# First batch's side steps moved to the side bank and VectorE, and the squares of the bound moved from GpSimd to ScalarE

## The chip, the cores and the metric

The kernel runs on one core of one Trainium2 chip, in a single launch. The metric is the device time of that launch in microseconds (us); less is better. A core has five engines with a queue each: TensorE (PE in the profile, with its weight loads as PEld), VectorE (DVE), ScalarE (ACT), GpSimd (POOL) and SyncE (SP), which only issues DMAs here. Each works through its own queue in program order and they meet through semaphores.

## What is computed

One transformer block over 4 sequences of 1024 tokens with 256 features, in float32: attention with 16 heads of 16, then a gated feed-forward with two hidden layers of 1024 and ternary weights. Cut to what matters:

```python
x = x + _layernorm(attn(_layernorm(x), Wqkv, Wout))
x = x + _layernorm(ffn(_layernorm(x), w1, s1, w2, s2, h1, ..., w3, s3))

def attn(x, Wqkv, Wout):
    q, k, v = split_heads(x @ Wqkv.T)                 # 16 heads of 16
    scores = einsum('bhqd,bhkd->bhqk', q, k) / 4
    e = exp(clip(scores - max(scores), -50, 50))
    return merge_heads((e / (sum(e) + 1e-6)) @ v) @ Wout.T

def ffn(x, ...):
    h = silu(x @ w1.T * s1) * (x @ w2.T * s2)
    h = gelu(h @ h1.T * hs1)
    h = gelu(h @ h2.T * hs2)
    return h @ w3.T * s3
```

The fast path takes the exponential without subtracting the maximum. It therefore also works out, for each batch, a bound on the scores from the squared norms of the rows of q and k, and counts a miss where that bound is too large. If anything was missed, a slow general path is run after the fast one.

## The kernel before, in words

**Stages.** Attention runs for batches 0 to 3, one after the other, and then the feed-forward for the eight half batches. In attention a batch has 4 groups of 4 heads, and 2 halves of 512 queries; a group and a half make a *unit* of 16 *tiles*. A tile (`exponentials`, lines 444 to 452) is two score matmuls of TensorE into one PSUM buffer `s` of 128x1024 (tag "big", three buffers), and one exponential of ScalarE from it into a ring. `weigh` (line 459) multiplies the exponentials with the values into the unit's accumulator `acc`; `rise` (line 468) keeps running maxima on VectorE.

**Turns.** The main loop (lines 858 to 878) goes by turns. In each, it issues the scores and exponentials of three new tiles, the maxima and the weighing of those of the turn before, and then calls `side.take()` once. `Side` (lines 551 to 578) holds chains of small steps. A call of `take` goes through all chains in order, and runs a chain's next step if as many turns have passed since its last step as the step's `gap` says. Steps marked as TensorE steps (the default) are limited to one per turn over all chains; others are free. So `gap` 0 means in the same turn as the step before, and `gap` 1 a turn later.

**The steps of a batch.** `prologue(b, space, copy)` (line 271) makes a batch's steps: normalising the rows (`gather`, `root`, `apply`), transposing them (`transposes`, line 305), projecting them to values (`values`, line 315) and to q and k (`project`, line 324), and the bound (`flags`, lines 334 to 393). Each of those that uses TensorE takes a PSUM place from `space(name)` and brings its result to SBUF by `copy`: `to_scalar` (line 266, on ScalarE) or `to_vector` (line 269, on VectorE). `project` makes two results of one product: `hi`, rounded, by `copy`, and `lo`, the rest, always on VectorE (line 328).

Two places are in use for these steps. `misc` is a single bank of its own (tag "misc", one buffer). The other is one of the three "big" buffers that the scores use. Batches 1 to 3 pass `misc` and `to_vector` (line 586): their steps run as side steps while the batch before is attended. Batch 0 passes a "big" buffer and `to_scalar` (line 819). Its normalising, transposing, its first q and k and `v[0]` run before the first tile, straight from lines 827 to 840; the rest (`v[1]` to `v[3]`, the second half of the features of q and k in four projections, and the flags) are side steps of the first units (lines 844 and 845). Between them stand the steps `slots`, in which GpSimd spreads the values into the layout `vaug` that `weigh` reads.

**The bound.** For each half of 512 tokens there are four squares (`kinds`: q and k, two blocks of features), each a product of a 128x512 `hi` with itself into a bfloat16 tile `sq` of four buffers, on GpSimd (line 338). `bound` (lines 354 to 361) sums them over the head's features by four matmuls, and VectorE takes maxima (`norm`). In the end `gauge` and `flag` compare. In the list of line 401 the squares have gap 0 and are no TensorE steps, so the four of a half are issued in one turn; `bound` follows three turns later at the earliest, when the turn's TensorE step is free.

**Other work in the same turns.** At the end of a unit VectorE copies the accumulator (`o`), and in the next turn `divide` (lines 470 to 493) takes one "big" buffer, transposes maxima and sums with TensorE and divides on VectorE. At the end of a batch `ending` projects the result and adds it to x. All through the first three batches `check_weights` (lines 237 to 263) checks that the feed-forward weights survive rounding: GpSimd loads and casts, VectorE counts (line 257). SyncE copies q and k into the stacked layout of the scores by DMA.

Of the kernel before, what the change touches and what calls it, by code (L numbers as in the profile page):

```python
# [9 lines left out]
F32 = mybir.dt.float32  # L10
# [3 lines left out]
AF = mybir.ActivationFunctionType  # L14
ALU = mybir.AluOpType
# [3 lines left out]
P = 128  # L19
# [16 lines left out]
NQ = 512  # L36
# [4 lines left out]
@with_exitstack  # L41
def tile_attention_ffn_block(ctx: ExitStack, tc: tile.TileContext, x, wqk, wv, wo, w1, w1s, w2, w2s, h1, h1s, h2, h2s, w3, w3s, out):

    nc = tc.nc
    B, S, D = x.shape
    bad = ctx.enter_context(tc.tile_pool(name="flag", bufs=1)).tile([1, 1], I32, name="bad")
    tile_fast(tc, x, wqk, wv, wo, w1, w1s, w2, w2s, h1, h1s, h2, h2s, w3, w3s, out, bad)
    failed = nc.values_load(bad[0:1, 0:1], min_val=0, max_val=1 << 24)
    with tc.If(failed > 0):
        tile_general(tc, x, wqk, wv, wo, w1, w1s, w2, w2s, h1, h1s, h2, h2s, w3, w3s, out)
# [46 lines left out]
def tile_fast(ctx: ExitStack, tc: tile.TileContext, x, wqk, wv, wo, w1, w1s, w2, w2s, h1, h1s, h2, h2s, w3, w3s, out, bad):  # L115
    nc = tc.nc
# [19 lines left out]
    def pieces(h, view):  # L136

        t, n = NH + (TPQ - 1) * h, TPQ * h
        return (slice(n, n + 1), view[:, h : h + 1, :]), (slice(n + 1, n + TPQ), view[:, t : t + TPQ - 1, :])

    def load_x(b, halves=range(NH)):
        view = x[b].rearrange("(t p) d -> p t d", p=P)
        for h in halves:
            for at, tokens in pieces(h, view):
                nc.sync.dma_start(out=xs[b][:, at, :], in_=tokens)
# [26 lines left out]
    ps = ctx.enter_context(tc.tile_pool(name="ps", bufs=3, space=PSUM))  # L172
# [4 lines left out]
    with ExitStack() as actx, ExitStack() as rctx:  # L177
# [56 lines left out]
        def misc(name):  # L234
            return ps_misc.tile([P, NQ], F32, tag="misc", name=name)
# [35 lines left out]
        def prologue(b, space, copy):  # L271
# [6 lines left out]
            def gather(h, i):  # L278
                def run():
                    if h == i == 0:  # L280
                        st["xT"] = work.tile([P, DC, S], F32, tag="xT", name=f"xT_{b}", bufs=1)
                    st["mv", h] = norms.gather(rows(h)[i : i + 2], i, st.get(("mv", h)))

                return run

            def root(h):
                def run():
                    st["ln", h] = norms.root(st["mv", h])

                return run  # L290

            def apply(h, i0):
                def run():
                    if i0 == 0:
                        st["xn"] = work.tile([P, TPQ, D], F32, tag="xn", name="xn", bufs=1)
                    for i in range(i0, i0 + 2):
                        norms.apply(st["xn"][:, i, :], rows(h)[i], st["ln", h], i)

                return run

            def transposes(h, c):
                def run():
                    pt = space(f"pt_{b}_{h}_{c}")
                    for i in range(TPQ):
                        nc.tensor.transpose(pt[:, i * P : (i + 1) * P], st["xn"][:, i, c * P : (c + 1) * P], ident)
                    copy(st["xT"][:, c, h * NQ : (h + 1) * NQ], pt)

                return run

            def values(t0):  # L310
                def run():
                    pv = space(f"pv_{b}_{t0}").rearrange("p (t d) -> p t d", d=D)
                    for i in range(2):
                        for c in range(DC):
                            nc.tensor.matmul(pv[:, i, :], st["xT"][:, c, (t0 + i) * P : (t0 + i + 1) * P], wv_sb[:, c, :], start=c == 0, stop=c == DC - 1)  # L315
                    copy(cv[:, t0 : t0 + 2, :], pv)

                return run

            def project(w, m, h):  # L320
                def run():
                    pp = space(f"p{w}_{b}_{m}_{h}")
                    for c in range(DC):
                        nc.tensor.matmul(pp, wqk_sb[:, c, w, HPT * m : HPT * (m + 1), :], st["xT"][:, c, h * NQ : (h + 1) * NQ], start=c == 0, stop=c == DC - 1)  # L324
                    hi, lo = (cq[w, m, k][:, h * NQ : (h + 1) * NQ] for k in ("hi", "lo"))
                    scale = 1.0 if w else 1.0 / math.sqrt(DH)
                    copy(hi, pp, scale)
                    nc.vector.scalar_tensor_tensor(lo, pp, scale, hi.bitcast(F32), ALU.mult, ALU.subtract)

                return run  # L330

            kinds = [(w, m) for w in range(2) for m in range(DC)]

            def squares(w, m, h):
                def run():
                    sq = st["sq", w, m] = work.tile([P, NQ], BF16, tag="sq", name="sq", bufs=4)
                    hi = cq[w, m, "hi"][:, h * NQ : (h + 1) * NQ].bitcast(F32)
                    nc.gpsimd.tensor_tensor(sq, hi, hi, ALU.mult)

                return run  # L340

            def total(m):
                def run():
                    if m == 0:
                        st["norm"] = work.tile([P, NT], F32, tag="norm", name=f"norm_{b}", bufs=1)
                        st["sum"] = work.tile([P, DC], F32, tag="sum", name="sum", bufs=1)
                        st["sum2"] = work.tile([P, DC], BF16, tag="sum2", name="sum2", bufs=1)
                    t = st["sum"][:, m : m + 1]
                    nc.vector.tensor_reduce(t, cq[1, m, "hi"].bitcast(F32), AX.X, ALU.add)
                    nc.gpsimd.tensor_tensor(st["sum2"][:, m : m + 1], t, t, ALU.mult)  # L350

                return run

            def bound(h):


                def run():
                    pn = space(f"pn_{b}_{h}")
                    for k, (w, m) in enumerate(kinds):
                        nc.tensor.matmul(pn[SLOT * k : SLOT * (k + 1), :], heads_bf, st["sq", w, m], start=True, stop=True)  # L360
                    nc.vector.tensor_reduce(st["norm"][:, TPQ * h : TPQ * (h + 1)], pn.rearrange("p (t n) -> p t n", n=P), AX.X, ALU.max)

                return run
# [31 lines left out]
            norm = [[Step(gather(h, i), 1, False) for i in range(0, TPQ, 2)] + [Step(root(h), 0, False)] for h in range(NH)]  # L395
            xt = [[Step(apply(h, i), 1, False) for i in range(0, TPQ, 2)] + [Step(transposes(h, c), 1) for c in range(DC)] for h in range(NH)]
            qk = [[[Step(project(w, m, h), 1) for w in (1, 0)] for h in range(NH)] for m in range(DC)]
            v = [Step(values(t), 1) for t in range(0, NT, 2)]
            flags = [Step(total(m), 1, False) for m in range(DC)]
            for h in range(NH):  # L400
                flags += [Step(squares(w, m, h), 0, False) for w, m in kinds] + [Step(bound(h), 3)]
            return norm, xt, qk, v, flags + [Step(gauge, 0, False), Step(flag, 1)]

        def copies(g, w, c0=0, c1=S):
# [14 lines left out]
        def stack(b, g):  # L419
            for w in (1, 0):  # L420
                for copy in copies(g, w):
                    copy(nc.sync)
            stacked[g % 2] = b, g
# [159 lines left out]
        def begin(b):  # L583

            if b + 1 < B:
                norm, xt, qk, v, flags = prologue(b + 1, misc, to_vector)

                qk1 = sum(qk[1], [])
                qk1[0].gap = 3
                later["rest"] = v, qk1 + [Step(lambda: side.add(flags), 0, False)]  # L590

                later["chain"] = side.add([Step(lambda: None, 0 if b else 4, False)] + sum((norm[h] + xt[h] for h in range(NH)), []) + sum(qk[0], []))
# [210 lines left out]
        def feed_forward():  # L803
# [12 lines left out]
                chain = side.add(finish(n, ffn["a"]), True)  # L816
            side.flush()

        norm, xt, qk, v, flags = prologue(0, lambda n: ps.tile([P, 2, NQ], F32, tag="big", name=n)[:, 0, :], to_scalar)

        queues = [nc.scalar] + [nc.gpsimd, nc.sync] * 3 + [nc.gpsimd]

# [15 lines left out]
                        step.run()  # L838
        stacked[0] = 0, 0
        v[0].run()  # L840
        load_x(1)
        stack(0, 1)
        load_rest()
# [14 lines left out]
        while weighed < len(tiles):  # L858
            n = made
            make(n + TURN - side.borrowed)  # L860
            if made == len(tiles):
                n = made
# [3 lines left out]
            while weighed + 2 <= n:  # L866
                b, g, h, c, _ = tiles[weighed]
# [252 lines left out]
```

## Time and profile before

| | us |
|---|---|
| median of three runs | 1350.21 (1348.44 to 1350.24) |
| the profiled execution | 1349.57 |
| its span, first to last instruction | 1347.8 |
| the stage before the first tile | 0 to 25 |
| attention | 25 to 671 |
| feed-forward | 671 to 1347.8 |

Busy times of the engines in these stages (us), from the table of stretches:

| stage | PE | DVE | ACT | POOL |
|---|---|---|---|---|
| 0 to 25 | 19.4 | 11.0 | 7.3 | 13.2 |
| 25 to 671 | 598.5 | 406.6 | 488.8 | 126.5 |
| 671 to 1347.8 | 661.5 | 318.4 | 189.0 | 19.5 |

The lines of the profile give a start, a length, an engine, the line of the program, the operation, what it writes and reads by the program's names, and how many like it were merged ("x6"). In brackets stands how long the engine had been idle before it, and what ended that. A busy TensorE isn't TensorE at its peak: the length of a matmul includes time in which it shares the array with the next. The squares in groups:

```profile
L338 POOL TENSOR_TENSOR sq<-cq1hi 128x512 bf16<-128x512 f32 x8 | 11.4, 1430 | 0.0
L338 POOL TENSOR_TENSOR sq<-ck0hi 128x512 bf16<-128x512 f32 x8 | 11.0, 1371 | 0.0
L338 POOL TENSOR_TENSOR sq<-ck1hi 128x512 bf16<-128x512 f32 x8 | 10.6, 1329 | 0.0
L338 POOL TENSOR_TENSOR sq<-cq0hi 128x512 bf16<-128x512 f32 x8 | 8.3, 1036 | 2.3 <-PE pn L360 2.3
```

Behind the bars stand the group's busy time in us, the mean of one in ns, and the idle time before them.

### The profile page before, as it was taken

To read this page: it belongs to the slowest core of one execution; us is meant where nothing else is said; L and a number is where in the kernel's file an instruction comes from. 1 tells how busy PE (TensorE), PEld (TensorE's weight loads), DVE (VectorE), ACT (ScalarE), POOL (GpSimd) and SP (SyncE) were. 2 spreads that over 40 slices of the span, in tenths; PEclk is the share of its full clock that TensorE was granted. 3 is DMA by queue.
4 is the path that set the end of the run, shared out by engine and by line. 5 is a ranking of instruction groups with operands and counts; after the bars stand their busy time and mean duration, and the time that the engine had idled before them with its cause. 6 is when DMAs were issued, how large, how long until landed. Compare 5 with 4: busy or idle time off the path is not lost.

```text
span 1347.8 us, 18771 instructions
## 1 busy us (share of the span) xinstructions
PE 1279.4 (95%) x7042; PEld 799.8 (59%) x7042; DVE 736.0 (55%) x1554; ACT 685.1 (51%) x822; POOL 159.2 (12%) x198
## 2 busy tenths in 40 slices
PE   7889999899899999989999999999999999999995
PEld 3333434333343434323378888888888888888885
DVE  3485568665697565735573453635537354362623
ACT  4576687676778678888842231413214142231410
POOL 6151133210521003000000000000000000000000
PEclk9999999899999999999999999999999999999998
DMA  4674344533445432236130000000000000000000
GB/s 132 150 176 113 78 111 93 141 90 69 130 104 141 95 50 49 48 65 198 36 153 1 1 16 0 17 1 0 16 1 16 1 1 17 0 16 1 17 0 19
DMA packets 38662, 79.62 MB, mean 59 GB/s; under 512 B 11296, under 2 KB 21152, under 8 KB 38560
## 3 DMA queue, kind: packets, MB, share of 16 engines
q1 hardware_dynamic: 30672, 53.66, 18.3%
q0 software_dynamic: 7360, 24.12, 5.4%
q8 instruction: 58, 0.95, 0.3%
q10 hardware_dynamic: 528, 0.52, 0.2%
q14 instruction: 44, 0.36, 0.1%
HBM read 28.98 MB, written 15.73 MB: 33 GB/s over the span
## 4 chain that ended last, share of the span: by engine, by line
PE 75%; DVE 12%; ACT 7%; issue 2%; POOL 2%; DMA 1%; SPq 1%; ACTq 0%; POOLq 0%; DVEq 0%
PE ph L697 35%; PE acc L459 13%; PE s L451 8%; ACT e L452 5%; PE pz L750 4%; PE p L324 4%; PE pg L697 3%; PE py L516 2%; PE pv L315 2%; DVE sg L713 2%; DVE top L468 2%; PE po L480 1%; DVE ha_lo L702 1%; DVE st L93 1%; DVE o L269 1%
## 5 line engine op out<-in xcount | busy, mean ns | idle before, releaser
L452 ACT ACTIVATE e<-s 128x1024 f32<-128x1024 f32 x512 | 484.9, 1033 | 144.4 <-PE s L451 128.5
L459 PE MATMUL acc<-e,vaug 128*32 128x512 f32 x2048 | 258.3, 607 | 1.8 <-POOL vaug L429 1.8
L733 ACT ACTIVATE a<-ph,h_scale 128x512 f32<-128x512 f32 x128 | 81.0, 685 | 306.9 <-PE ph L697 306.9
L451 PE MATMUL s<-sq,sk 64*128 64x512 f32 x1024 | 196.4, 453 | 26.1 <-ACT e L452 20.4
L697 PE MATMUL ph<-hb_lo,h 128*128 128x512 f32 x512 | 199.4, 389 | 0.0
L697 PE MATMUL ph<-hb_hi,h 128*128 128x512 f32 x512 | 199.4, 389 | 0.0
L451 PEld LDWEIGHTS s<-sq,sk 64*128 64x128 f32 x1024 | 87.5, 186 | 162.8 <-ACT e L452 120.1
L468 DVE TENSOR_TENSOR top<-top,e 128x512 f32<-128x512 f32 x192 | 146.2, 761 | 30.1 <-ACT e L452 24.1
L103 POOL TENSOR_TENSOR rstd<-ve,minus_half 128x4 f32<-128x4 f32 (+1 forms) x33 | 37.5, 1135 | 796.5 <-DVE ve L101 796.5
L459 PEld LDWEIGHTS acc<-e,vaug 128*32 128x32 f32 x2048 | 49.6, 109 | 108.8 <-issue 98.5
L734 DVE CAST ha_hi<-a 128x512 fp32r<-128x512 f32 x64 | 27.1, 424 | 157.9 <-ACT a L733 157.9
L697 PEld LDWEIGHTS ph<-hb_lo,h 128*128 128x128 f32 x512 | 96.1, 188 | 20.1
L697 PEld LDWEIGHTS ph<-hb_hi,h 128*128 128x128 f32 x512 | 96.1, 188 | 20.1
L697 PE MATMUL ph<-ha_hi,sq 128*128 128x512 f32 x256 | 101.9, 398 | 0.4
L697 PE MATMUL ph<-ha_lo,sq 128*128 128x512 f32 x256 | 99.8, 390 | 0.0
L697 PE MATMUL ph<-ha_lo,sk 128*128 128x512 f32 x256 | 99.7, 390 | 0.0
L697 PE MATMUL ph<-ha_hi,sk 128*128 128x512 f32 x256 | 99.7, 390 | 0.0
L713 DVE SCALAR_TENSOR_TENSOR sg<-pg,w_scale,sg 128x512 f32<-128x512 f32 x64 | 47.1, 745 | 47.9 <-ACT sg L711 47.8
L711 ACT ACTIVATE sg<-pg,w_scale 128x512 f32<-128x512 f32 x64 | 43.3, 688 | 56.6 <-DVE ha_lo L702 48.4
L734 DVE CAST hb_hi<-a 128x512 fp32r<-128x512 f32 x64 | 27.0, 422 | 82.2 <-ACT a L733 82.2
L324 PE MATMUL p<-xT,wqk_sb 128*128 128x512 f32 x128 | 64.6, 631 | 1.2 <-ACT xT L266 1.2
L697 PEld LDWEIGHTS ph<-ha_hi,sq 128*128 128x128 f32 x256 | 48.2, 188 | 12.7 <-DVE sg L713 3.4
(147 smaller groups left out, 1689.7 us busy)
## 6 DMA issues: line engine op xcount, KB each, us to landing
w<-in_h_dram POOLq DMA_DIRECT2D x16, 512.0 KB, 4.7
h_r<-wr POOLq DMA_DIRECT2D x16, 512.0 KB, 3.6
sk<-ck1hi SPq DMA_DIRECT2D x64, 64.0 KB, 2.3
sk<-ck1lo SPq DMA_DIRECT2D x64, 64.0 KB, 2.3
sq<-cq1hi SPq DMA_DIRECT2D x64, 64.0 KB, 2.3
sq<-cq1lo SPq DMA_DIRECT2D x64, 64.0 KB, 2.3
h<-h_r SPq DMA_DIRECT2D x8, 512.0 KB, 6.5
sk<-ck0hi SPq DMA_DIRECT2D x56, 64.0 KB, 2.3
```

Of the source, the lines that this page charges most:

```text
L103: nc.gpsimd.tensor_tensor(rstd[:, :n], ve[:, :n], self.minus_half[:, :n], ALU.pow)
L324: nc.tensor.matmul(pp, wqk_sb[:, c, w, HPT * m : HPT * (m + 1), :], st["xT"][:, c, h * NQ : (h + 1) * NQ], start=c == 0, stop=c == DC - 1)
L451: nc.tensor.matmul(s[:, a, :], stacks[1, g % 2, u][r, c * P : (c + 1) * P], stacks[0, g % 2, u][r, h * NQ : (h + 1) * NQ], start=True, sto ...
L452: nc.scalar.activation(pair(k)[:, u], s, AF.Exp)
L459: nc.tensor.matmul(acc[SLOT * i : SLOT * (i + 1), :], vaug[g % 2][:, c, i, :], pair(k)[:, i // 2, i % 2, :], start=c == 0, stop=c == NT - 1)
L468: nc.vector.tensor_max(top, top if c > 1 else pair(k - 2)[:, :, :, 0:P], pair(k)[:, :, :, 0:P])
L697: nc.tensor.matmul(p, homes[n][c][:, m * P : (m + 1) * P], half[:, c, :], start=c == 0 and k == 0, stop=c == len(homes[n]) - 1 and k == 1)
L711: nc.scalar.activation(sg, p[:, 0, :], AF.Silu, scale=scales["w1"][:, m : m + 1])
L713: nc.vector.scalar_tensor_tensor(sg, p[:, 1, :], scales["w2"][:, m : m + 1], sg, ALU.mult, ALU.mult)
L733: nc.scalar.activation(a, p[:, j, :], AF.Gelu, scale=scales[n][:, m : m + 1])
L734: nc.vector.tensor_copy(o[0][:, m, :], a)
L750: nc.tensor.matmul(p[t], half[:, c, t * P : (t + 1) * P], homes["w3"][c], start=c == 0 and k == 0, stop=c == HC - 1 and k == 1)
```

## The change

Two things are changed. Batch 0 gets a `space` and a `copy` that look at a switch, `alone`, when a step is run: as long as it is set they are the "big" buffer and ScalarE as before, and from the point after `v[0]` on they are `misc` and VectorE, as for the other batches. The squares of all batches become an activation `Square` of ScalarE with the same input and output, and their gaps change from 0 to 1, so that a half's four squares are issued in four turns; the gap of `bound` changes from 3 to 1.

```diff
@@ squares (line 338)
-                    nc.gpsimd.tensor_tensor(sq, hi, hi, ALU.mult)
+                    nc.scalar.activation(sq, hi, AF.Square)
@@ the list of the flags (line 401)
-                flags += [Step(squares(w, m, h), 0, False) for w, m in kinds] + [Step(bound(h), 3)]
+                flags += [Step(squares(w, m, h), 1, False) for w, m in kinds] + [Step(bound(h), 1)]
@@ batch 0's steps (line 819)
-        norm, xt, qk, v, flags = prologue(0, lambda n: ps.tile([P, 2, NQ], F32, tag="big", name=n)[:, 0, :], to_scalar)
+        alone = True
+
+        def first_space(name):
+            return ps.tile([P, 2, NQ], F32, tag="big", name=name)[:, 0, :] if alone else misc(name)
+
+        def first_copy(*args):
+            (to_scalar if alone else to_vector)(*args)
+
+        norm, xt, qk, v, flags = prologue(0, first_space, first_copy)
@@ after line 840
         v[0].run()
+        alone = False
         load_x(1)
```

## The prediction

> **What bounds the kernel now.** I read the page first. TensorE is busy 95% of the span and the second half is the feed-forward, which the change doesn't touch. So only the attention stage counts; its last exponential (the group of line 452) starts at 670.1 us.
>
> ```profile
> PE   7889999899899999989999999999999999999995
> ...
> PEclk9999999899999999999999999999999999999998
> ...
> L452 ACT ACTIVATE e<-s 128x1024 f32<-128x1024 f32 x512 | 484.9, 1033 | 144.4 <-PE s L451 128.5
> ```
>
> The third line says that ScalarE sits idle 144 us before exponentials, nearly all for scores from TensorE: neither engine bounds the whole stage, the turn decides. The timeline shows three sorts of turn. In a light one (no TensorE side step) six exponentials run in 5.61 us without a gap, so ScalarE sets the pace at 0.92 us each. After a divide, and in turns with a projection, ScalarE waits for scores:
>
> ```profile
> 183.13 5.61 ACT L452 ACTIVATE e<-s 128x1024 f32<-128x1024 f32 x6 [0.19 <-PE s L451]
> ...
> 189.53 1.94 ACT L452 ACTIVATE e<-s 128x1024 f32<-128x1024 f32 x2 [0.80 <-PE s L451]
> ```
>
> In the first batch a projection borrows a score buffer; the third score pair of the next turn waits until its copies are done:
>
> ```profile
> 46.82 0.74 PE L451 MATMUL s<-sq,sk 64*128 64x512 f32 x4
> ...
> 46.93 0.60 ACT L266 ACTIVATE ck1hi<-p 128x512 fp32r<-128x512 f32 x1 [1.07 <-PE p L324]
> ...
> 48.31 0.49 PE L451 MATMUL s<-sq,sk 64*128 64x512 f32 x2 [0.75 <-DVE ck1lo L328]
> ...
> 48.73 1.92 PE L459 MATMUL acc<-e,vaug 128*32 128x512 f32 x16
> ```
>
> The next view, of 75 to 135 us, holds two things. The squares on GpSimd run from 77.49; the VectorE operations beside them take double, and the divide at 83.11 waits 3.31 us for the last of these. At 107.08 the second batch's projection, in the side bank, shows the same turn without a borrowed buffer.
>
> ```profile
> 76.80 2.27 DVE L468 TENSOR_TENSOR top<-top,e 128x512 f32<-128x512 f32 x2
> ...
> 77.49 1.04 POOL L338 TENSOR_TENSOR sq<-cq0hi 128x512 bf16<-128x512 f32 x1
> ...
> 80.07 1.45 DVE L257 SCALAR_TENSOR_TENSOR w<-w,wr 128x512 f32<-128x512 f32 x1
> ...
> 83.11 0.63 PE L478 MATMUL po<-ident,top 128*128 128x128 f32 x4 [3.31 <-DVE top L468]
> ...
> 107.08 0.98 PE L451 MATMUL s<-sq,sk 64*128 64x512 f32 x6
> ...
> 107.98 1.92 PE L459 MATMUL acc<-e,vaug 128*32 128x512 f32 x16
> ```
>
> The second batch's squares do it again, to a row scaling that takes 0.72 us for two elsewhere:
>
> ```profile
> 235.44 2.17 DVE L111 TENSOR_SCALAR y<-y,mv,rstd 128x256 f32<-128x256 f32 x2
> ...
> 238.88 1.12 PE L305 MATMUL pt<-ident,xn 128*128 128x128 f32 x4 [3.39 <-DVE xT L269]
> ```
>
> Last, the table of stretches (columns: length, busy PE, PEld, DVE, ACT, POOL, then the clock): after each such stall the granted clock is about half.
>
> ```profile
> 80.00:84.00 4.00, 0.89 (x7) 0.80 (x8) 3.56 (x5) 1.33 (x2) 4.00 (x5) 1.00 0.60 101
> 84.00:88.00 4.00, 4.00 (x23) 1.13 (x21) 3.38 (x11) 1.94 (x2) 0.65 (x2) 0.57 0.96 267
> ...
> 240.00:244.00 4.00, 4.00 (x18) 1.35 (x22) 2.61 (x5) 2.85 (x3) 1.04 (x1) 0.50 0.61 164
> ```
>
> **What the Trainium skill says.** "GPSIMD Engine Reference", section 8: GpSimd shares its SBUF interfaces with VectorE and collides with instructions that have two SBUF inputs or use a 2-port mode. The trace agrees: two maxima 1.41 us alone, 2.27 beside squares. "TensorE: Matmul & The Clock Gate", Part 1: an idle window of about 3.4 us halves the clock; the trace has 0.57 after a stall of 3.31. "ScalarE: Activation LUTs", Table sets: cheap functions such as copy and relu are in every set; Square isn't in that list by name, and no run here shows one. The trace's table loads are at lines 155 (the start), 711 and 733, none around the copies of line 266.
>
> **The change: first batch's steps.** From v[1] on, the steps use the one side bank and VectorE. Seven PSUM copies move: ScalarE loses 7 x 0.60 = 4.2 us, VectorE gains 7 x 0.69 = 4.8. No DMA moves.
> - Four projections: first score to first acc takes 1.91, 2.08, 1.90, 1.91 us now, 0.90 in the side bank. Worth 1.0 each, but the third is followed by a divide that waits for VectorE (1.09 us at 61.56), which must now do "hi" (0.69) before "lo": nothing there. So 3.0.
> - v: the last copy goes behind three maxima that end at 42.90; 42.90 + 0.69 + 0.62 for the slot copy on GpSimd puts acc at 44.27 instead of 43.91. Loss 0.4, and the stall of about 0.45 in the turn before is eaten by it: minus 0.4.
> - Bounds and flag: the score wait on the norm at 91.03 (0.63), and six score matmuls in 1.60 instead of 0.96 us at 151.98: 0.9 together.
> The sum is 3.5 us. Behind each waiting VectorE copy stand the maxima of the next turn, which nobody needs before the end of a unit. Bounds: 0 if VectorE stays late, 6 if nothing does.
>
> **Squares off GpSimd.** 32 squares (8 each at about 1.04, 1.43, 1.37, 1.33 us) leave it. VectorE wins at 76.8 to 83.1: 0.86 (maxima), 0.77 (the count at 0.68 elsewhere), 0.8 (the last maximum, 1.51); of these 2.4 I take 1.6 as shortening the wait of 3.31, because VectorE enters only 2.0 us earlier where TensorE is 2.5 ahead. Second batch, second half: 1.45 + 0.7 = 2.1 of the wait of 3.39. Third batch: maxima at 2.36 and a count at 1.51 before a divide that waits 1.81 with ScalarE idle 3.16: 2.3. Where ScalarE runs without a gap (182 to 188, 504 to 509) nothing is won. Also the second batch's norm, gauge and flag (0.68 + 0.22 + 1.2 us of VectorE) now come after its divide of 251.74, which waits 1.68: 1.6. With 0.2 for the rest, 7.8; bounds 3 and 10.
> The half-rate stretches after the stalls cost, row by row against the same groups at full clock, 1.5 us (acc 2.91 for 1.92, scores 1.22 for 0.73), 2.6 (after 238.88) and 1.3 (after 251.74): 5.4. A stall of 1.81 us at 354.62 left the clock at 1.00, so shorter stalls should save it. I take half, 2.7; bounds 0 and 5.4.
>
> **Squares on ScalarE.** A square is 128x512: the nearest row, the copy of line 266, takes 600 ns; "ScalarE: Activation LUTs", What ACT_TABLE_LOAD costs, gives 186 + 0.833 x 512 = 612 ns and 93 ns of overlap. So it costs 0.52 us in a turn that ScalarE bounds, and nothing in an idle gap of that size. Which turns? Each call of the side planner is one turn: each chain runs what its gap allows, one TensorE step per turn in all. Counting from the lists, before has the squares at turns 10, 13 / 36, 50 / 77, 80 / 120, 123; after has them at 11-14, 23-26 / 38-41, 51-54 / 78-81, 87-90 / 121-124, 135-138. What runs beside them:
> - Batch 0: 11 and 12 lie in the gap before the divide (3.80 us idle now), 13 and 14 are light but follow VectorE: 0.6. 23-26 have a divide and three v steps (idle 1.28 to 1.87): 0.
> - Batch 1: 38 is light, 39 a divide (0.80 idle), 40 and 41 out-projection transposes (0.58 and 0.74 idle, one of two hidden): 0.8. 51-54 sit beside stalls of 3.79 and 1.99: 0.8.
> - Batch 2: 78-80 light, 81 a divide; part lies in the idle 3.16: 1.2. 87-90 divide, two transposes, a projection: 0.3.
> - Batch 3: 121-123 light: 1.5. 136-138 light: 1.3.
> Sum 6.5. Bounds: 2.5 (five in full), 16.6 (32 x 0.52). The exponentials of the next turn queue behind a square, and acc behind these; the bound's matmuls run a turn later, so they find it done. In the first batch the m = 0 squares of the second half (turns 23 and 25) come after the next batch's projections (18 to 21) and read those rows; the wait for that is long over, it costs no time.
>
> **Sum.** 3.5 + 7.8 + 2.7 - 6.5 = 7.5 us. The profiled execution took 1349.57 (span 1347.8 and 1.8 around it), so 1342.1; the median of the runs is 0.6 higher: 1342.7.
>
> **Rivals.**
> - Nothing to see (within 0.2%, 2.7 us, about what a measurement of this kernel can tell from no change): the first batch's gain ends at its first two divides, where VectorE is late anyway (busy 13.86 of 16 us from 75 to 91), and half rate comes at other places. Then 4 + 0.5 + 3 - 6.5 = 1 us: 1349. For it: VectorE gets 4.8 us more just before; against: its slow operations there are GpSimd's doing.
> - Slower: ScalarE pays for every square, because scores are released by exponentials, so a delay there passes to TensorE even in turns that I call covered. 32 x 0.52 = 16.6 against 11.3 without the clock's part: plus 5.3, 1355.5. It decides from about 22 paid squares on. For it: ScalarE's gapless groups; against: gaps of 0.58 to 1.87 us in the divide and projection turns.
> - Square in another table set: two loads per square, 64 x 1.28 = 82 us, 1432. Against: the copies need none.
>
> **How the numbers follow.** Forecast, faster by over 2.7 us: 0.63, own range 1337 to 1347. No difference: 0.18. Slower by over 2.7: 0.19 (0.18 squares, 0.01 tables). The range 1336 to 1353 leaves out some 0.06 below and 0.12 above.
>
> **What would show it.** Right: no square on GpSimd, 32 on ScalarE near 0.6 us; seven more copies at line 269; no score wait on "lo" of the first batch; TensorE's wait for the maxima before divides (10.6 us, longest 3.3) falls by half; the clock near 86 and 242 us is full; the last exponential near 663 us. Wrong: gapless exponentials with squares between them in turns 23-26 or 39-41, new divide waits of over 2 us in the first 90 us, a table load between exponentials.

## The result and the profile after

The changed kernel takes 1335.63 us (median of 4 runs, 1335.24 to 1335.79), the kernel before beside it 1349.97 (4 runs, 1348.44 to 1350.24). The ratio is 0.9896, with a 95% interval of 0.9879 to 0.9913. The profiled execution took 1335.65 us, its span 1333.7 instead of 1347.8. The forecast had said 1342.7, in a range from 1336.0 to 1353.0: right in direction, but the gain is 14.3 us instead of 7.5, and the time lies just under the range.

The last exponential starts at 656.3 us instead of 670.1. So 13.8 of the 14.1 us of span were won in attention. The same three lines of the page as before, of the changed kernel:

```profile
PE   7999999999999999989999999999999999999996
...
PEclk9999999999999999999999999999999999999998
...
L452 ACT ACTIVATE e<-s 128x1024 f32<-128x1024 f32 x512 | 486.3, 1036 | 131.1 <-PE s L451 117.8
```

ScalarE's wait for scores fell from 128.5 to 117.8 us, although ScalarE also has the squares now. These are their groups in the changed kernel (busy us, mean ns, idle before):

```profile
L338 ACT ACTIVATE sq<-ck1hi 128x512 bf16<-128x512 f32 x8 | 5.4, 680 | 0.0
L338 ACT ACTIVATE sq<-cq0hi 128x512 bf16<-128x512 f32 x8 | 5.3, 667 | 0.0
L338 ACT ACTIVATE sq<-ck0hi 128x512 bf16<-128x512 f32 x8 | 5.2, 655 | 0.0
L338 ACT ACTIVATE sq<-cq1hi 128x512 bf16<-128x512 f32 x8 | 5.2, 648 | 0.0
```

All 32 stand on ScalarE, none on GpSimd, and no table load stands between exponentials. TensorE's waits in the changed kernel, from 20 to 680 us (total, times, longest):

```profile
PE po L478 <- DVE top L468: 5.5, 9, 2.2
...
PE acc L459 <- POOL vaug L429: 2.9, 2, 1.9
...
PE pt L305 <- DVE xT L269: 1.2, 1, 1.2
```

Before, the first was 10.6 us (12 times, longest 3.3), the last 3.4 us; the second was 1.8 and has grown, as the prediction's loss for v has it. The waits of scores on `lo` of the first batch, 3.0 us together, are gone altogether. Now the place of the first batch's squares, which was quoted from 76.80 on in the kernel before:

```profile
73.70 1.48 DVE L468 TENSOR_TENSOR top<-top,e 128x512 f32<-128x512 f32 x2
74.81 0.68 ACT L338 ACTIVATE sq<-cq0hi 128x512 bf16<-128x512 f32 x1
...
76.17 0.66 DVE L257 SCALAR_TENSOR_TENSOR w<-w,wr 128x512 f32<-128x512 f32 x1
...
77.59 0.63 PE L478 MATMUL po<-ident,top 128*128 128x128 f32 x4 [0.88 <-DVE top L468]
```

Two maxima take 1.48 us instead of 2.27, the count 0.66 instead of 1.45, and the divide waits 0.88 us instead of 3.31. The same stretch of the second batch:

```profile
227.03 0.73 DVE L111 TENSOR_SCALAR y<-y,mv,rstd 128x256 f32<-128x256 f32 x2
...
229.03 0.66 PE L305 MATMUL pt<-ident,xn 128*128 128x128 f32 x4 [1.22 <-DVE xT L269]
...
237.80 0.66 PE L478 MATMUL po<-ident,top 128*128 128x128 f32 x4
```

The row scaling takes 0.73 us instead of 2.17, the transposes wait 1.22 instead of 3.39. And the stretches of which two ran at a clock near a half before (columns as before; the clock is the third number from the end):

```profile
84.00:88.00 4.00, 3.17 (x26) 0.98 (x22) 3.31 (x7) 4.00 (x6) 0.90 (x2) 1.00 0.78 209
240.00:244.00 4.00, 3.81 (x30) 1.19 (x28) 3.90 (x13) 3.30 (x4) 0.15 (x1) 1.00 0.77 222
```

Both show 1.00. The mean clock of the execution is 0.994 instead of 0.988.

**Where the time came from.** The start of the first exponential of every unit (16 tiles, 8 units per batch) was read from both traces. The third column is what the steps of the prediction add up to in that stretch, with half of each half-rate stretch as the sum has it:

| stretch, in the time of before | won (us) | the prediction's steps |
|---|---|---|
| start to unit 2 (77.0) | 3.1 | 2.6 |
| to unit 3 (99.1): first squares | 3.7 | 2.4 |
| to unit 6 (165.5) | 2.0 | 0.5 |
| to unit 9 (223.5) | -1.1 | -0.8 |
| to unit 11 (266.3): second batch's second squares | 7.2 | 4.8 |
| to unit 16 (372.9) | 1.3 | 1.1 |
| to unit 24 (530.3) | -1.4 | -1.8 |
| to the last exponential (670.1) | -1.0 | -1.3 |

Gains and losses fall where they were expected. The sizes differ most in three rows: the two in which half-rate stretches vanished, and the one from 99 to 165 us. With these stretches counted whole instead of half, the two rows would read about 3.2 and 6.8.

In the first row two other half-rate stretches nearly cancel, and the prediction has neither: one at 33.0 us, which the changed kernel lacks, and one at 59.3, which the kernel before lacks. Other runs below show what each costs. squares_only has the instructions of the kernel before up to unit 2, but no half rate at 33.0, and is 1.7 us faster from its first tile to there. pool_spread and double_square have those of the changed kernel up to unit 2, but no half rate at 59.3, and win 1.6 us more from unit 1 to unit 2.

### The profile page after: what moved, and what is told of

The parts are those of the page before. It is cut to its first block, busy times and chain, and to the rows that moved or that the text cites. A ratio compares the mean times of both kernels' runs of the same rounds, so it can differ in the third digit from the quotient of the medians.

```text
span 1333.7 us, 18779 instructions
## 1 busy us (share of the span) xinstructions
PE 1271.8 (95%) x7042; PEld 797.1 (60%) x7042; DVE 724.3 (54%) x1561; ACT 696.6 (52%) x847; POOL 120.7 (9%) x166
## 4 chain that ended last, share of the span: by engine, by line
PE 78%; DVE 9%; ACT 7%; issue 2%; POOL 1%; DMA 0%; SPq 0%; ACTq 0%; POOLq 0%; DVEq 0%
PE ph L697 35%; PE acc L459 13%; PE s L451 8%; ACT e L452 6%; PE pg L697 6%; PE pz L750 4%; PE p L324 4%; PE py L516 2%; PE pv L315 2%; DVE top L468 2%; PE po L480 1%; DVE o L269 1%; DVE sg L713 1%; DVE st L93 1%; DVE ha_lo L702 1%
## 5 line engine op out<-in xcount | busy, mean ns | idle before, releaser
L452 ACT ACTIVATE e<-s 128x1024 f32<-128x1024 f32 x512 | 486.3, 1036 | 131.1 <-PE s L451 117.8
L468 DVE TENSOR_TENSOR top<-top,e 128x512 f32<-128x512 f32 x192 | 134.1, 699 | 35.7 <-ACT e L452 30.1
```

Source lines behind the costliest of these rows:

```text
L452: nc.scalar.activation(pair(k)[:, u], s, AF.Exp)
L468: nc.vector.tensor_max(top, top if c > 1 else pair(k - 2)[:, :, :, 0:P], pair(k)[:, :, :, 0:P])
```

## The experiments

"Units" below means this reading of the exponentials' starts, in us earlier than in the kernel before; the changed kernel has 3.1 at unit 2, 8.8 at unit 6, 14.8 at unit 11 and 13.8 at the end. Each group of runs had its own runs of the kernel before.

**One half of the change at a time.** steps_only keeps the first batch's new place and engine, and puts the squares back:

```diff
-                    nc.scalar.activation(sq, hi, AF.Square)
+                    nc.gpsimd.tensor_tensor(sq, hi, hi, ALU.mult)
-                flags += [Step(squares(w, m, h), 1, False) for w, m in kinds] + [Step(bound(h), 1)]
+                flags += [Step(squares(w, m, h), 0, False) for w, m in kinds] + [Step(bound(h), 3)]
```

> Only the first batch's steps are moved; squares on GpSimd, four in a turn. Theory A (three separate causes: borrowed score buffers, GpSimd's squares slowing VectorE, half clock after the stalls): gains only the first, 3.5 to 5 us, so 1345 to 1346.5, and the half-rate stretches between 238 and 255 us stay. Rival B (the first batch's gain comes from the squares and the flags leaving its crowded turns, not from the buffers): within 2 us of before, 1348 to 1351.

Measured: 1348.67 us (20 runs, 1342.56 to 1353.05) against 1349.73, ratio 0.9992 (0.9978 to 1.0005); the profiled execution's span is 1342.5. The median is the rival's. But the units show the steps' gain: 3.4 at unit 2, as in the changed kernel and with the same half-rate stretches up to there, then 2.3 at unit 3 where the changed kernel has 6.8. The squares on GpSimd take it back there, and the clock with them:

```profile
80.00:84.00 4.00, 4.00 (x20) 2.18 (x23) 2.34 (x9) 1.55 (x2) 0.77 (x2) 0.50 0.86 220
84.00:88.00 4.00, 3.87 (x24) 0.96 (x16) 2.81 (x8) 1.64 (x3) 2.29 (x2) 0.75 0.77 195
```

In its 20 runs the time goes with the mean granted clock: 1342.56 us at 0.992, 1353.05 at 0.982, a straight line of -1008 us per unit of clock (correlation -0.986). How much of the gain is kept depends, it seems, on how often a stall is followed by half rate. Of the stretches between 238 and 255 us that theory A expected to stay, the profiled execution has one, at 236.2.

squares_only is the kernel before with `Square` on ScalarE and gaps of 1 and 1, and the first batch's steps as they were.

> Only the squares are moved to ScalarE, one per turn; the first batch's steps as before. Theory A: the rest of the gain, about 10 us, 1339 to 1341, no half-rate stretch between 230 and 260 us. Rival B: 13 us or more, 1334 to 1337.

Measured: 1340.05 us (1339.51 to 1340.46), ratio 0.9931 (0.9915 to 0.9948). The squares carry most of the gain: 13.0 at unit 11. The changed kernel is 1.8 us ahead at unit 24, which is what the first batch's steps add, net of the half rate at 59.3 us that squares_only lacks. Later squares_only loses 1.6 us more in a half-rate stretch at 587.5, which no other trace has.

**Is it the engine, or one square per turn?** In act_together all four squares of a half stay in one turn (gap 0, bound 3), on ScalarE; in pool_spread they stay on GpSimd, one per turn:

```diff
 act_together
-                flags += [Step(squares(w, m, h), 1, False) for w, m in kinds] + [Step(bound(h), 1)]
+                flags += [Step(squares(w, m, h), 0, False) for w, m in kinds] + [Step(bound(h), 3)]
 pool_spread
-                    nc.scalar.activation(sq, hi, AF.Square)
+                    nc.gpsimd.tensor_tensor(sq, hi, hi, ALU.mult)
```

> The changed kernel with the squares on ScalarE but four in one turn (gap 0, bound three turns later). Theory A (what matters is that GpSimd no longer runs beside VectorE): within 3 us of the changed kernel, 1334 to 1339. Rival C (what matters is the spreading, which also takes the norm, gauge and flag out of the turns before a divide): 1342 or more.

Measured: 1351.88 us (13 runs, 1348.99 to 1352.76), ratio 1.0013 (1.0005 to 1.0022). The whole gain is gone: 5.8 at unit 11, -1.2 at unit 24. ScalarE's timeline in this kernel:

```profile
348.24 0.64 ACT L338 ACTIVATE sq<-cq0hi 128x512 bf16<-128x512 f32 x1
348.76 0.64 ACT L338 ACTIVATE sq<-cq1hi 128x512 bf16<-128x512 f32 x1
349.28 0.64 ACT L338 ACTIVATE sq<-ck0hi 128x512 bf16<-128x512 f32 x1
349.80 0.64 ACT L338 ACTIVATE sq<-ck1hi 128x512 bf16<-128x512 f32 x1
350.32 4.69 ACT L452 ACTIVATE e<-s 128x1024 f32<-128x1024 f32 x5
```

For 2.08 us no exponential starts, and five without a gap after it show that ScalarE is behind from there on.

> The changed kernel with the squares back on GpSimd but one per turn. Theory A: each square still slows one or two VectorE operations by 0.7 us, but a single one can be absorbed before a divide; half of the squares' gain, 1338 to 1343. Rival C: as fast as the changed kernel or faster by ScalarE's 6 us, 1329 to 1336.

Measured: 1338.07 us (1337.17 to 1341.6), ratio 0.9921 (0.9901 to 0.994). One square per turn, with GpSimd kept, gives most of the gain: 10.1 at unit 6, where the changed kernel has 8.8. That lead is the missing half rate at 59.3 us; from unit 2 to unit 6 the two win 5.8 and 5.7. It loses at one place, units 9 to 11, where it wins 1.8 us and the changed kernel 7.2:

```profile
227.52 3.92 DVE L468 TENSOR_TENSOR top<-top,e 128x512 f32<-128x512 f32 x1
227.85 1.05 POOL L338 TENSOR_TENSOR sq<-cq0hi 128x512 bf16<-128x512 f32 x1
228.85 1.04 POOL L338 TENSOR_TENSOR sq<-cq1hi 128x512 bf16<-128x512 f32 x1
229.85 1.03 POOL L338 TENSOR_TENSOR sq<-ck0hi 128x512 bf16<-128x512 f32 x1
...
240.41 1.09 PE L478 MATMUL po<-ident,top 128*128 128x128 f32 x4 [1.72 <-DVE top L468]
```

Three squares, issued in three turns, start back to back here; one maximum beside them takes 3.92 us instead of 0.69. The transposes at 240.41 take 1.09 instead of 0.66: the clock is a half again.

So one per turn in the program is not one per turn on GpSimd: in two more halves, from 492.87 and from 546.20, all four squares follow each other. Nor does VectorE lose less time. Counting its instructions beside squares that took over 1.25 times the median of their kind, the excess adds up to about 20 us here and 16 in the kernel before. The difference is where it falls. In the first batch one square starts at 76.69, with the divide at 76.59, and the other three behind it; in the kernel before all four ran ahead of the divide at 83.11.

**Bank or engine, for the first batch.** bank_scalar uses the side bank but copies with ScalarE; big_vector keeps the score buffer and copies with VectorE:

```diff
 bank_scalar
-            (to_scalar if alone else to_vector)(*args)
+            to_scalar(*args)
 big_vector
-            return ps.tile([P, 2, NQ], F32, tag="big", name=name)[:, 0, :] if alone else misc(name)
+            return ps.tile([P, 2, NQ], F32, tag="big", name=name)[:, 0, :]
```

> The changed kernel, but the first batch's side steps, in the side bank, are copied by ScalarE. Theory A (the gain is the score buffer that is no longer borrowed): as the changed kernel within 1.5 us, 1334 to 1337. Rival D (the gain is that ScalarE's copies of 0.60 us no longer stand ahead of exponentials): 3 to 4 us slower, 1338.5 to 1340.

Measured: 1336.32 us (1335.45 to 1338.03), ratio 0.9908 (0.9891 to 0.9924); units within 0.5 us of the changed kernel throughout.

> The changed kernel, but the first batch's side steps keep a score buffer, and are copied by VectorE. Theory A: loses the first batch's part, 3 to 5 us slower than the changed kernel, 1338.5 to 1341. Rival D: as the changed kernel within 1.5 us.

Measured: 1338.58 us (1338.26 to 1340.9), ratio 0.9924 (0.9908 to 0.9941); 0.4 at unit 2 instead of 3.1, and 3.4 behind at the end. In the side bank, then, the copying engine makes no difference that shows, and the bank is worth 3.4 us, with a half-rate stretch at 59.3 that big_vector lacks. squares_only is the fourth case, a score buffer copied by ScalarE. From the first tile to unit 2 it is 1.2 us faster than big_vector, and neither has a half-rate stretch there: with a borrowed buffer VectorE's copies are the worse ones.

**The price of a square on ScalarE.** double_square issues each one twice; no_square leaves the squares out, and the bound reads a tile of zeros.

```diff
 double_square
                     nc.scalar.activation(sq, hi, AF.Square)
+                    nc.scalar.activation(sq, hi, AF.Square)
 no_square
-                    nc.scalar.activation(sq, hi, AF.Square)
+                    st["sq", w, m] = one_sq
```

> The changed kernel with each of the 32 squares done twice on ScalarE. Theory A (about 13 of the 32 fall in turns that ScalarE bounds): plus 6 to 8 us, 1341.5 to 1343.5. Rival E (a square is paid wherever it stands): plus 16 us or more, 1352. Rival F (squares are hidden): plus 2 us or less.

Measured: 1345.93 us (8 runs, 1344.6 to 1350.65), ratio 0.9986 (0.9971 to 1.0); 4.8 at the end, so in the profiled execution, the fastest of the eight, the second 32 squares cost 9.0 us. By the ratios of the medians it is 12. Both are more than theory A's 6 to 8 and less than rival E's 16.

> The changed kernel without the squares: the bound's matmuls read a tile of zeros, so the score bound isn't computed. Theory A: minus 5 to 7 us, 1329 to 1331. Rival E: minus 14 us or more, 1321. Rival F: minus 2 us or less, 1333.5 to 1336.

Measured: 1337.71 us (1335.67 to 1338.52), ratio 0.9916 (0.9899 to 0.9932). It isn't faster, because its first tile came 3.5 us late, and that is the experiment's own doing. VectorE has to clear the tile of zeros, waits for a copy of ScalarE before it does, and begins to normalise the first rows only behind it, at 10.21 us instead of 2.76:

```profile
10.02 0.27 DVE L234 MEMSET sq<- 128x256 uint32 x1 [7.79 <-ACT wqk_sb L187]
```

From unit 1 to the end it wins 14.8 us, the changed kernel 11.2. So the first 32 squares cost about 3.7 us, less than theory A's 5 to 7: by the units 0.5 in the first batch, 0.7 in the second, 0.7 in the third and 1.7 in the fourth.

**Why four at once cost so much.** act_late_four runs the four squares in the turn of the last one, so that the bound and the flag keep their turns:

```diff
-                flags += [Step(squares(w, m, h), 1, False) for w, m in kinds] + [Step(bound(h), 1)]
+                flags += [Step(squares(w, m, h), 0 if k else 4, False) for k, (w, m) in enumerate(kinds)] + [Step(bound(h), 1)]
```

> The changed kernel with a half's four squares in one turn on ScalarE, in the turn in which the changed kernel has the fourth, so that the bound and the flag stay in their turns. Theory G (four squares in a row hold up the exponentials by 2.1 us, and TensorE, without work, drops to half clock): 8 to 16 us slower than the changed kernel. Rival H (four in a turn was slow because the bound and the flag came in crowded turns before a divide): within 2 us of the changed kernel.

Measured: 1339.64 us (1338.59 to 1339.93), ratio 0.9925 (0.9906 to 0.9944), against 1334.66 (1333.56 to 1337.79) for the changed kernel in the same group of runs. That is 5.0 us, between the two expectations; a half-rate stretch at 411.2 us, which the changed kernel lacks, is part of it. Of the 16 us that act_together loses, bunching explains 5. Its trace has three half-rate stretches more than the changed kernel's, 2.5 to 3.8 us by the two lines through runs below, and one of them may be in the 5 already. The rest may come with its bound and flag in earlier turns; the runs didn't separate that.

> The changed kernel once more, as the measure for the three others of this call: 1334 to 1338.

Measured: the changed kernel a second time, ratio 0.9895 (0.9874 to 0.9916), with every unit within 0.3 us of the first.

**Is it GpSimd's burst by itself?** dead_pool is the changed kernel, with the same four products of a half done by GpSimd as well, at the turn of the first square, into memory that nobody reads:

```diff
+                    if (w, m) == kinds[0]:
+                        for v, n in kinds:
+                            x = cq[v, n, "hi"][:, h * NQ : (h + 1) * NQ].bitcast(F32)
+                            nc.gpsimd.tensor_tensor(w3s_sb.bitcast(BF16), x, x, ALU.mult)
```

> The changed kernel, and besides GpSimd squares the same four inputs in one burst into a tile that nobody reads, at the turn of a half's first square (the row scales w3s are loaded later, to make room for that tile). Nothing waits for the burst but GpSimd's own later work. Theory A (the burst slows VectorE, and the stalls bring the half clock back): 5 to 12 us slower than the changed kernel, VectorE operations of twice their length beside the burst. Rival H (only the order of the steps mattered): within 2 us.

Measured: 1343.31 us (1342.46 to 1344.41), ratio 0.9953 (0.9934 to 0.9971), 8.65 more than the changed kernel beside it. No result of these products is waited for, and yet the old picture is back (its line numbers are 3 higher from line 341 on):

```profile
231.29 1.05 POOL L341 TENSOR_TENSOR w3s_sb<-cq0hi 128x512 bf16<-128x512 f32 x1
...
232.82 2.25 DVE L111 TENSOR_SCALAR y<-y,mv,rstd 128x256 f32<-128x256 f32 x2
...
242.91 1.09 PE L481 MATMUL po<-ident,top 128*128 128x128 f32 x4 [2.74 <-DVE top L471]
```

and in the table of stretches the half clock, from 241.9 us on:

```profile
244.00:248.00 4.00, 4.00 (x21) 1.55 (x23) 3.00 (x10) 1.94 (x2) 0.84 (x2) 0.50 0.82 219
```

The scaling takes 2.25 us (2.17 before, 0.73 after), the divide waits 2.74. Between this burst and the divide VectorE waits for nothing from GpSimd. So here the cause is what GpSimd does to VectorE beside it, and not a wait for the squares.

This place is most of the price. By the units the burst costs 5.1 us from unit 9 to 11 and 1.1 from unit 16 to 17, and the other bursts next to nothing. Of the 8.3 us between the two profiled executions at the last exponential, 2.0 were lost before the first burst, most of it with a half-rate stretch at 33.5 us. And in the first batch the burst starts at 79.73, just behind the divide at 79.63, and the 3.7 us from unit 2 to unit 3 stay won; pool_spread wins 3.9 there. In this place the later turn is enough by itself, GpSimd could have kept the squares, and rival H is right.

**Squares on both engines.** mixed_squares leaves them on ScalarE in the first two batches, and gives them to GpSimd, one per turn, in the last two.

```diff
-                    nc.scalar.activation(sq, hi, AF.Square)
+                    if b < 2:
+                        nc.scalar.activation(sq, hi, AF.Square)
+                    else:
+                        nc.gpsimd.tensor_tensor(sq, hi, hi, ALU.mult)
```

> The changed kernel with the squares of batches 2 and 3 on GpSimd, one per turn, those of 0 and 1 on ScalarE. By the times of single units in the runs so far the squares cost ScalarE 1.2, 0.7 and 1.2 us in batches 2 and 3, and GpSimd's, spread, nothing there: 3 us faster than the changed kernel, 1331 to 1334. If the half clock comes back in one of these places: no gain, or slower.

Measured: 1335.08 us (6 runs, 1333.48 to 1337.15), ratio 0.9895 (0.9879 to 0.9911). From unit 2 to the end it wins 12.9 us, the changed kernel 10.7, but it loses 2.1 us of that up to unit 2, where its instructions are still the same and its profiled execution has a half-rate stretch at 33.2 us. That it beats the changed kernel isn't shown.

## Why the prediction was right in direction and too small

The span gained 14.05 us where the sum had 7.5, a difference of 6.55. The mechanism held, with one exception in the first batch; two terms of the sum were mis-sized, the clock's and the squares' price on ScalarE. Term by term:

**First batch's steps (3.5 predicted): right.** squares_only, which has the old steps, is 1.8 us behind at unit 24; with the 1.6 us put back that the half rate at 59.3 cost the changed kernel, the steps gain about 3.4. The details hold too. Scores of a projection turn now run as in the other batches:

```profile
45.23 0.96 PE L451 MATMUL s<-sq,sk 64*128 64x512 f32 x6
45.33 0.69 DVE L269 TENSOR_SCALAR ck1hi<-p 128x512 fp32r<-128x512 f32 x1 [3.54 <-PE p L324]
...
46.12 1.92 PE L459 MATMUL acc<-e,vaug 128*32 128x512 f32 x16
...
57.86 0.63 PE L478 MATMUL po<-ident,top 128*128 128x128 f32 x4 [2.20 <-DVE top L468]
```

Six scores go through in one piece, and the weighing starts 0.89 us after them (1.91 before). After the third projection the gain is nothing, as said: the divide at 57.86 waits 2.20 us for VectorE, where it waited 1.09. The prediction had named "new divide waits of over 2 us in the first 90 us" as a sign against itself. One such wait came, a half-rate stretch follows it, and the total still won.

**Squares off GpSimd (7.8 predicted): right, as far as a remainder can tell.** Together with the first batch's steps the sum had 11.3 us. The measured gain, with the squares' price put back and the clock's part taken off, is 14.05 + 3.7 minus 3.4 to 6.8 (below), so 11.0 to 14.4. That is what is left over, not a measurement. If there is an excess, 1.5 us of it lies from 99 to 165 us, the prediction's "0.2 for the rest": squares_only wins 1.3 us there. dead_pool shows the cause directly in the second batch. In the first, the prediction credits the engine with what the turn alone does as well: its own count moves the squares from turn 10 to turns 11 to 14, and dead_pool's burst, from turn 11 on, cost nothing.

**The half-rate stretches ("I take half, 2.7; bounds 0 and 5.4"): the first term that failed.** The prediction saw 5.4 us in the stretches after the stalls, argued that shorter stalls should save them, and took half all the same, without a reason. All of them went: after 84.2, 237.8 and 251.4 us the changed kernel has none. Counted from the trace, the kernel before has six windows of 3.41 us at half rate in its span ahead of the end (12.5, 33.0, 84.2, two at 237.8, 251.4), the changed kernel two (11.5, 59.3). A window lowers the mean clock of the run by 3.41 x 0.5 / 1347 = 0.00127. By the line through the runs of steps_only that is 1.28 us; by a line through 54 runs of the kernel before (-664 us per unit) it is 0.84. Four windows: 3.4 to 5.1 us. The two windows that could be priced directly, at 33 and 59 us, cost 1.5 to 1.7 each: 1.7 by squares_only against the kernel before, 1.5 and 1.7 by mixed_squares and dead_pool against the changed kernel, 1.6 by pool_spread and double_square. If the other four cost as much, they are 6.0 to 6.8 us. That is an estimate; the prediction's own 5.4 for the whole lies between the two.

**Squares on ScalarE (6.5 predicted): the second term that failed.** A square was put at 612 ns and measures 648 to 680; in a row they start every 0.52 us, as taken. Where they meet gapless exponentials, they stand as foreseen:

```profile
329.09 0.65 ACT L338 ACTIVATE sq<-cq0hi 128x512 bf16<-128x512 f32 x1
329.61 2.89 ACT L452 ACTIVATE e<-s 128x1024 f32<-128x1024 f32 x3
332.32 0.68 ACT L338 ACTIVATE sq<-cq1hi 128x512 bf16<-128x512 f32 x1
332.84 2.91 ACT L452 ACTIVATE e<-s 128x1024 f32<-128x1024 f32 x3
```

A turn takes 3.23 us from square to square, 0.52 over its exponentials. Yet no_square shows 3.7 us for all of them, not 6.5. By batch the prediction has 0.6, 1.6, 1.5 and 2.8; the runs show 0.5, 0.7, 0.7 and 1.7. At turns 40 and 41 (185.3 to 189 us) exponentials run without a gap between two squares, where the prediction had one of the two hidden; it had named that as a sign of being wrong, and the second batch still cost less than its 1.6. I think that part of a delay in light turns is made up at the next divide, where ScalarE waits for scores anyway; that was not tried by itself. double_square fits it: the second 32 squares, with less room left, cost 9.0.

So the 6.55 are made up of 2.8 for the squares, 0.7 to 4.1 for the clock, and what is left, 3.1 to nearly nothing, for the first two terms. Both failed terms err to the cautious side, so that they add up instead of cancelling.

**One stretch stays open.** From unit 6 to unit 9 the changed kernel loses 1.1 us where the prediction has 0.8 for squares. But no_square loses 1.0 there too, and pool_spread 1.0; so it is not the squares' price. The gaps of the flags are common to all three; which step does it wasn't tried.

**The rivals.** "Slower" needed about 22 squares paid in full; 3.7 / 0.52 is 7. "Nothing to see" needed late divides and moved half-rate stretches: both came once, at 57.86, which was too little. No tables were loaded. What no rival held is that the gap of 1 decides as much as the engine: act_together has the same engine and gains nothing, pool_spread the other engine and gains 11.7 us.

## What to carry to other kernels

When one engine's instructions become two to three times longer, look for what another engine does in the same stretch before looking at the waits: taking GpSimd's bursts away, or moving them behind the divide that waits for VectorE, won more here than the borrowed buffer. Small work for an engine that is close to its limit should be given out one piece per turn, since four pieces at once cost 5 us more than four pieces apart, one half-rate stretch included. And count a stall of TensorE with the half-rate window that may follow it.

## What the runs showed of the hardware

- A VectorE operation can stretch far beyond double beside GpSimd: one maximum took 3.92 us beside three squares, 0.69 alone. Of the collision "GPSIMD Engine Reference", section 8, in the Trainium skill tells the cause and no size.
- Half rate comes in pieces of 3.41 us or twice that in all fourteen traces, apart from a last one that begins 8 to 11 us before the end. In each trace they begin and end on one grid of 3.41 us, as "TensorE: Matmul & The Clock Gate", Part 1, says of a free-running window. But that part names an idle window as the trigger, and ahead of the changed kernel's stretch in attention TensorE was not idle for one (columns as before):

```profile
55.90:59.30 3.40, 1.44 (x12) 1.13 (x12) 2.58 (x8) 1.19 (x2) 2.53 (x3) 1.00 0.52 100
59.30:62.70 3.40, 3.40 (x20) 0.59 (x16) 2.62 (x8) 1.94 (x2) 0.00 (x0) 0.50 0.89 290
```

TensorE had been busy 1.44 of 3.40 us when the clock fell. The fourteen traces have 5400 windows of this grid at full rate. All 37 in which TensorE was busy under 1.48 us were followed by half rate, so were 15 of the 66 from 1.48 to 2.26, and none of the 5297 with more. (Busy times are as the profile models them.) Where a stall lies against the grid decides, too. In the kernel before, a stretch of 3.4 us with 1.61 us busy (351.2 to 354.6, the stall that the prediction argued from) lies across two windows with 2.36 and 2.50, and the clock stayed. The divide after the third projection, at 57.86 in the changed kernel, stands in ten traces with the same instructions around it: in seven its window has 1.22 to 1.59 us busy and half rate follows, in three it has 1.74 to 2.04 and none does. The measurement goes ahead of the page: a wait of 2 us can be enough.
- One and the same kernel spread over 10.5 us by its granted clock (steps_only). A comparison of two versions by a few runs each can miss a gain of 5 us; the starts of the units in the trace tell where it went.
